# Layer 0 self attention: the causal mask is added on VectorE inside the instruction that takes the maximum, instead of by a product on TensorE, and the score units are regrouped

## The chip, the cores and the metric

One core of a Trainium2 chip runs the whole decoder in one launch. The metric is the device time of that launch in microseconds (us). The engines are called by their names in the profile: PE (TensorE), DVE (VectorE), ACT (ScalarE), POOL (GpSimd), SP (which here only issues DMAs).

## The reference

The program is a two-layer decoder on x[4, 1024, 256]; each layer has self attention, cross attention and a feed-forward part, each with a residual and a layer normalisation. The change lies in the first of these six parts:

```python
def _L0_attn_ref(x, w_in, b_in, w_out, b_out):       # E = 256, H = 16 heads of 16
    q, k, v = jnp.split(x @ w_in.T + b_in, 3, axis=-1)
    q, k, v = (to_heads(q), to_heads(k), to_heads(v))
    scores = jnp.einsum('bhqd,bhkd->bhqk', q * scale, k) + causal_bias   # 0 or -inf
    attn = jax.nn.softmax(scores, axis=-1)
    out = jnp.einsum('bhqk,bhkd->bhqd', attn, v)
    return out.transpose(0, 2, 1, 3).reshape(bsz, slen, esz) @ w_out.T + b_out
x = _layernorm(x + _L0_attn_ref(x, ...))
```

The softmax needs, for every query, the largest score among the keys that the query may see.

## The kernel before, in words

The self attention (`self_attention`) works through 16 head groups s: four batches of four groups, four heads each. K and Q of a group are spread by DMAs over 128 partitions, 32 for each head (16 rows of data), so that a matmul of one head uses 32 rows of PE and the four heads can run beside each other.

Each group is computed twice over. In the first pass (**a units**, tile `s<-kp,qp`) the scores are made with queries on the partitions, only to take the maximum of every query row, on DVE. `highest` (L356) joins a group's partial maxima `nmp` into `nmt` with the sign turned, `shifted_queries` (L366, L370) transposes `nmt` on PE and adds it to the spread queries as one more row, so that the second pass (**b units**, tile `s<-qs,kp`) yields scores from which the maximum has been subtracted. ACT takes exp of these (L399), POOL zeroes what lies above the diagonal (L402), and `weighted` multiplies with the values (tile `acc<-p,v`). `normalised`, `turned_back` and `out_projected` finish a batch.

The causal mask in the a units: for a query block qc of 128 rows, keys up to qc x 128 are needed whole, and the diagonal block of 128 x 128 with a mask that is 0 on and below the diagonal and -1e30 above. Before the change, `a_units` lists seven units without diagonal blocks, and two more units (u = 7 and 8) hold four diagonal blocks each:

```python
def after():
    for g in range(2):
        mm(t[g], ident_bf, cmask4.rearrange("p j n -> p (j n)"), False, True)
    for g in range(2):
        nc.vector.tensor_reduce(
            nmp[:, 2 * pair + g, q0 : q0 + 4, 0], t[g].rearrange("p (j n) -> p j n", j=4),
            AX.X, ALU.max,
        )
```

So the mask is added in PSUM by a product of the identity with four copies of the mask (bf16, 512 columns), and one reduction (L348) takes four maxima. The other units' maxima are taken by L332, one reduction for each piece of a PSUM bank: one of 512 columns (u = 0 to 3), or two of 384 + 128, 256 + 256 or 128 + 384 (u = 4 to 6). In this document a **split step** is one with such a unit of two pieces, a **full step** one with a single product of 512 columns.

The order of the work is written out by hand: `at(when, f, ...)` notes an event, and `run_in_order` runs them by their time, which only orders them. A group has 18 steps (9 units, two pairs of heads); `together` issues one a unit of group s and one b unit of group s - 1 for the other pair of heads, round by round, so that four matmuls of 32 rows stand next to each other. Before the change a group starts with its four diagonal steps, then come eight full and six split steps; the values products, transposes and projections stand between the steps. PE's instructions keep this order (`keep_in_program_order`); the other engines' instructions are ordered by the scheduler.

PSUM: the tiles `s` come from a pool of seven banks in rotation (`bank()`). Each step takes four (two for the a unit, two for the b unit), and each transpose, projection or values product one more. The outputs' projection (`out_projected`) leaves DVE a chain of five short instructions (L478, L481, L482, L136, L137) and, for every fourth block, the layer normalisation (L152, L169).

Of the kernel before, what the change touches and what calls it, by code (L numbers as in the profile page):

```python
# [8 lines left out]
F32 = mybir.dt.float32  # L9
BF16 = mybir.dt.bfloat16  # L10
U8 = mybir.dt.uint8
AF = mybir.ActivationFunctionType
ALU = mybir.AluOpType
AX = mybir.AxisListType
PSUM = bass.MemoryType.PSUM

P = 128
# [4 lines left out]
NC = S // P  # L22
# [7 lines left out]
def decoder_kernel(ctx: ExitStack, tc: tile.TileContext, a: dict, out: bass.AP):  # L30
    nc = tc.nc
# [60 lines left out]
    ident_bf = const.tile([P, P], BF16, tag="ident_bf", name="ident_bf")  # L92
# [3 lines left out]
    cmask = const.tile([P, P], BF16, tag="cmask", name="cmask")  # L96
# [89 lines left out]
    def self_attention(wk, pss, psa):  # L186
        def pe(ins):
            tc.keep_in_program_order(ins)

        def mm(o, l, r, start, stop):  # L190
            pe(nc.tensor.matmul(o, l, r, start=start, stop=stop))  # L191

        def bank():
            return pss.tile([P, 512], F32, tag="s", name="s")

        bq4 = wk.tile([P, 2], F32, tag="bq4", name="bq4", bufs=1)
        nc.vector.tensor_scalar(bq4, l0a_bq, 0.25, None, ALU.mult)
        cmask4 = wk.tile([P, 4, P], BF16, tag="cmask4", name="cmask4", bufs=1)
        for i in range(4):
            nc.vector.tensor_copy(cmask4[:, i, :], cmask)  # L200

        row16 = wk.tile([P, 1], F32, tag="row16", name="row16", bufs=1)
        nc.vector.tensor_reduce(
# [13 lines left out]
        for i in range(2):  # L217
            vt = wk.tile([P, NC, 17 * H + 16], F32, tag=f"v{i}", name=f"v{i}", bufs=1)
            nc.gpsimd.memset(vt, 1.0)
            vts.append(vt)  # L220
            nmp = wk.tile([P, 4, NC, 3], F32, tag=f"nmp{i}", name=f"nmp{i}", bufs=1)
            nc.gpsimd.memset(nmp, -3.0e38)
            nmps.append(nmp)
            nmt = wk.tile([P, NC, 4, 32], F32, tag=f"nmt{i}", name=f"nmt{i}", bufs=1)
            nc.gpsimd.memset(nmt, 0.0)
            nmts.append(nmt)

        bo2 = wk.tile([P, E], F32, tag="bo2", name="bo2", bufs=1)
        t = bank()
# [6 lines left out]
        def at(when, f, *args):  # L236
            events.append((when, len(events), f, args))
# [55 lines left out]
        def spread(kind, s):  # L293
# [8 lines left out]
        a_units = [  # L302
# [7 lines left out]
        ]  # L310

        def a_unit(s, u, pair):

            t = [bank() for _ in range(2)]
            qt, kt, nmp = qpads[s % 2], kpads[s % 3], nmps[s % 2]
            rows = [slice(64 * pair + 32 * g, 64 * pair + 32 * g + 32) for g in range(2)]
            rounds = []
            if u < 7:
                for qc, k0, n, c0 in a_units[u]:
                    rounds.append([  # L320
                        (
                            t[g][:, c0 : c0 + n], qt[rows[g], qc * P : (qc + 1) * P],
                            kt[rows[g], k0 : k0 + n], True, True,
                        )
                        for g in range(2)
                    ])

                def after():
                    for g in range(2):
                        for qc, k0, n, c0 in a_units[u]:  # L330
                            i = 2 if k0 else 1
                            nc.vector.tensor_reduce(  # L332
                                nmp[:, 2 * pair + g, qc, i : i + 1], t[g][:, c0 : c0 + n], AX.X, ALU.max
                            )
            else:
                q0 = 4 * (u - 7)
                for j in range(4):
                    cols = slice((q0 + j) * P, (q0 + j + 1) * P)
                    rounds.append([
                        (t[g][:, j * P : (j + 1) * P], qt[rows[g], cols], kt[rows[g], cols], j == 0, False)  # L340
                        for g in range(2)
                    ])

                def after():
                    for g in range(2):
                        mm(t[g], ident_bf, cmask4.rearrange("p j n -> p (j n)"), False, True)
                    for g in range(2):
                        nc.vector.tensor_reduce(  # L348
                            nmp[:, 2 * pair + g, q0 : q0 + 4, 0], t[g].rearrange("p (j n) -> p j n", j=4),
                            AX.X, ALU.max,  # L350
                        )

            return rounds, after

# [135 lines left out]
        for b in range(NB):  # L490
# [9 lines left out]
            for c in range(NC):  # L500
                u = (117.5, 135.5, 151.5, 155.5, 157.5, 171.5, 175.5, 177.5)[c]
# [13 lines left out]
        for s in range(4 * NB):  # L515
# [9 lines left out]
            for i, place in ((0, 6), (4, 14), (5, 16), (7, 22)):  # L525
                qh, kc = (0, 0) if i == 0 else (1, i - 3)
                n = 512 if (place + 1) % T in full[(s + 1 + place // T) % 4] else 384
# [13 lines left out]
        for s in range(4 * NB + 2):  # L541
            for j in range(18):
                units = []
                if s < 4 * NB:
                    units.append((a_unit, s, (7, 8, 0, 1, 2, 3, 4, 5, 6)[j // 2], 1 - j % 2))

                sb, jb = divmod(18 * (s - 1) + j - 2, 18)
                if 0 <= sb < 4 * NB:
                    units.append((b_unit, sb, jb // 2, jb % 2))
                if units:  # L550
                    at(s * T + 1 + j, together, *units)
# [3 lines left out]
    with (  # L555
        tc.tile_pool(name="l0a", bufs=2, reuse_waits="tile") as wk,
        tc.tile_pool(name="ps_l0a", bufs=7, space=PSUM, reuse_waits="tile") as pss,
        tc.tile_pool(name="ps_l0o", bufs=1, space=PSUM, reuse_waits="tile") as psa,
    ):
        self_attention(wk, pss, psa)  # L560
# [1093 lines left out]
```

## Time and profile before

| | |
|---|---|
| three runs | 2245.08, 2246.88 (median), 2253.66 us |
| the profiled execution | 2244.4 us |
| its span, first to last instruction | 2244.4 us |
| mean granted PE clock | 0.983 |
| layer 0 self attention | about 30 to 735 us of the span |
| period of a head group there (L356 to L356, mean of 15) | 42.75 us |
| one split or full step on PE, where nothing holds it | 1.07 us |
| L332, 512 / 384 / 256 / 128 columns | 684 / 550 / 416 / 282 ns, 640 instructions |
| L348, four maxima over 512 columns | 686 ns, 128 instructions |
| mask product on PE (96 of 128 recorded) | 392 ns each |

How to read it: the page's first part gives each engine's busy time as a share of the span. The groups of instructions name line, engine, operation, tiles (written <- read), shapes, count, busy time and the mean of one, and then the engine's idle time before them with what ended it. In the timeline, instructions of one kind that follow each other are merged: "1.42 ... x4" is four of them from the first start to the last end, and the bracket is the idle time of that engine just before, with its releaser. A DVE instruction is shown with its full duration, although the next may start some 80 ns before it ends. PE's ends are modelled, so steps are measured here from the start of one to the start of what follows.

### The profile page before, as it was taken

How to read it: one execution, taken by the hardware profiler on the slowest of the kernel's cores; microseconds unless marked ns; L12 is line 12 of the kernel's file. 1: busy time of each engine (PE TensorE's matmuls, PEld its weight loads, DVE VectorE, ACT ScalarE, POOL GpSimd, SP SyncE). 2: the span in 40 equal slices, each digit the busy share in tenths (PEclk: the TensorE clock that was granted, in tenths of full speed). 3: DMA queues.
4: the chain of work that ended last, by engine and by line, in shares of the span. 5: the costliest groups of instructions: out<-in, count | busy, mean ns of one | idle time of the engine just before them, and what ended most of it. 6: DMA issues, size and time to landing. Idle time of an engine off the chain costs nothing.

```text
span 2244.4 us, 38974 instructions
## 1 busy us (share of the span) xinstructions
PE 2120.4 (94%) x14676; PEld 1269.1 (57%) x14708; DVE 1492.5 (66%) x3287; ACT 1121.5 (50%) x2861; POOL 508.1 (23%) x1113
## 2 busy tenths in 40 slices
PE   7999999999999899999999998989999999999996
PEld 4544555554554556556556555666666655565554
DVE  5666667767775655558997887886973465555644
ACT  1455554555555365546756654454542234545443
POOL 1111111111111354444444443000000121111111
PEclk9999999999999999999999999999999999999998
DMA  4101100000000100000000000000000010010101
GB/s 115 34 6 53 39 6 16 15 11 15 11 11 1 39 1 20 1 1 1 1 1 1 34 1 22 0 1 1 1 1 1 2 20 15 15 29 10 29 1 37
DMA packets 24443, 34.83 MB, mean 16 GB/s; under 512 B 5952, under 2 KB 19648, under 8 KB 24256
## 3 DMA queue, kind: packets, MB, share of 16 engines
q1 hardware_dynamic: 22640, 31.20, 6.0%
q8 instruction: 116, 1.90, 0.3%
q10 hardware_dynamic: 1616, 1.16, 0.2%
q14 instruction: 71, 0.58, 0.1%
HBM read 15.56 MB, written 4.19 MB: 9 GB/s over the span
## 4 chain that ended last, share of the span: by engine, by line
PE 71%; DVE 19%; ACT 6%; issue 1%; POOL 1%; DMA 1%; SPq 0%; ACTq 0%; POOLq 0%; DVEq 0%
PE s L191 20%; PE t L590 16%; PE s L1190 10%; PE s L590 8%; PE acc L191 6%; DVE gt L940 4%; PE acc L1190 3%; PE t L774 2%; ACT u L749 2%; DVE nmp L332 2%; DVE x L169 1%; DVE nmx L745 1%; DVE bnst L136 1%; DVE ht L926 1%; DVE gt L950 1%
## 5 line engine op out<-in xcount | busy, mean ns | idle before, releaser
L399 ACT ACTIVATE p<-s 128x512 f32<-128x512 f32 x576 | 312.2, 595 | 292.4 <-PE s L191 284.2
L332 DVE TENSOR_REDUCE nmp<-s 128x1 f32<-128x512 f32 (+3 forms) x640 | 298.8, 523 | 153.7 <-PE s L191 152.9
L191 PE MATMUL s<-qs,kp 32*128 32x512 f32 (+3 forms) x1536 | 348.3, 522 | 0.0
L191 PE MATMUL s<-kp,qp 32*128 32x128 f32 (+3 forms) x2304 | 325.3, 404 | 2.4 <-DMA qp<-sq 2.1
L757 POOL TENSOR_SCALAR p<-u,rs 128x128 f32<-128x128 f32 x512 | 214.7, 437 | 292.3 <-DVE rs L753 199.9
L191 PEld LDWEIGHTS s<-kp,qp 32*128 32x128 f32 x2304 | 163.4, 187 | 135.2 <-ACT p L399 46.2
L402 POOL TENSOR_SCALAR_AFFINE_SELECT p<-p 128x256 f32<-128x256 f32 x256 | 99.5, 407 | 562.9 <-ACT p L399 562.9
L749 ACT ACTIVATE u<-s,nmx 128x154 f32<-128x154 f32 x512 | 192.0, 388 | 31.9 <-DVE nmx L745 27.9
L154 POOL TENSOR_TENSOR rstd<-ve,neghalf 128x4 f32<-128x4 f32 (+1 forms) x56 | 56.9, 1016 | 582.2 <-DVE ve L152 578.1
L191 PE MATMUL acc<-p,v 128*32 128x384 f32 (+3 forms) x2016 | 167.9, 420 | 0.1
L191 PEld LDWEIGHTS s<-qs,kp 32*128 32x128 f32 x1536 | 139.0, 184 | 29.1 <-DVE nmp L332 8.5
L590 PEld LDWEIGHTS s<-kt,qt 64*128 64x128 f32 x1024 | 102.5, 188 | 71.5 <-issue 53.6
L590 PE MATMUL s<-kt,qt 64*128 64x154 f32 x1024 | 136.2, 316 | 0.5 <-ACT qt L731 0.3
L590 PE MATMUL t<-xT,xw 128*128 128x512 f32 x256 | 123.2, 604 | 12.2 <-DVE xT L677 8.4
L745 DVE TENSOR_REDUCE nmx<-s 128x4 f32<-128x616 f32 x128 | 101.3, 791 | 48.4 <-PE s L590 48.2
L1347 DVE TENSOR_REDUCE nmt<-s 128x3 f32<-128x462 f32 (+1 forms) x192 | 99.0, 579 | 45.2 <-PE s L1190 45.1
L590 PE MATMUL t<-v,pt 128*128 128x256 f32 x512 | 118.0, 384 | 7.0 <-DVE pt L1099 7.0
L940 DVE SCALAR_TENSOR_TENSOR gt<-ht,cw,gt 128x256 f32<-128x256 f32 x256 | 116.9, 500 | 5.5 <-ACT gt L936 4.8
L590 PE MATMUL t<-xw,ot 128*128 128x256 f32 x512 | 116.3, 381 | 3.7 <-ACT pr L778 1.7
L590 PE MATMUL s<-qt,xT 128*128 128x512 f32 x256 | 116.8, 600 | 0.0
L590 PEld LDWEIGHTS t<-v,pt 128*128 128x128 f32 x512 | 97.0, 192 | 29.6 <-DVE pt L1099 8.1
L348 DVE TENSOR_REDUCE nmp<-s 128x4 f32<-128x512 f32 x128 | 82.4, 686 | 41.2 <-PE s L191 35.8
(259 smaller groups left out, 3892.2 us busy)
## 6 DMA issues: line engine op xcount, KB each, us to landing
qp<-sq SPq DMA_DIRECT2D x128, 64.0 KB, 2.4
kp<-sk SPq DMA_DIRECT2D x64, 64.0 KB, 2.3
out_dram<-x SPq DMA_DIRECT2D x8, 512.0 KB, 2.9
x<-in_x_dram SPq DMA_DIRECT2D x3, 1024.0 KB, 5.6
wf<-in_L_ffn_w_dram SPq DMA_DIRECT2D x2, 1024.0 KB, 6.0
xw<-in_L_xattn_wk_dram SPq DMA_DIRECT2D x1, 1024.0 KB, 6.4
xw<-in_L_xattn_wq_dram SPq DMA_DIRECT2D x1, 1024.0 KB, 5.0
xw<-in_L_xattn_wv_dram SPq DMA_DIRECT2D x1, 1024.0 KB, 5.0
```

Source lines behind the costliest of these rows:

```text
L191: pe(nc.tensor.matmul(o, l, r, start=start, stop=stop))
L332: nc.vector.tensor_reduce(nmp[:, 2 * pair + g, qc, i : i + 1], t[g][:, c0 : c0 + n], AX.X, ALU.max)
L348: nc.vector.tensor_reduce(nmp[:, 2 * pair + g, q0 : q0 + 4, 0], t[g].rearrange("p (j n) -> p j n", j=4), AX.X, ALU.max,)
L399: nc.scalar.activation(p[:, g, :], t[g], AF.Exp)
L402: nc.gpsimd.affine_select(out=v, in_=v, compare_op=ALU.is_ge, fill=0.0, base=0, pattern=[[0, 2], [1, P]], channel_multiplier=-1,)
L590: pe(nc.tensor.matmul(o, l, r, start=start, stop=stop))
L745: nc.vector.tensor_reduce(nmx.rearrange("p i g -> p g i"), t, AX.X, ALU.max, negate=True)
L749: nc.scalar.activation(u[:, 2 * i + g, :], t[:, g, i, :], AF.Exp, bias=nmx[:, i, g : g + 1], accum_out=ssum[:, i, g : g + 1],)
L757: nc.gpsimd.tensor_scalar(p[:, h * P : (h + 1) * P], u[:, h, :P], rs[:, h : h + 1], 1.0, ALU.mult, ALU.mult)
L940: nc.vector.scalar_tensor_tensor(g, ht[:, i, k : k + N], cw[:, hc, k : k + 1], g, ALU.mult, ALU.add)
L1190: pe(nc.tensor.matmul(o, l, r, start=start, stop=stop))
L1347: nc.vector.tensor_reduce(nmts[s % 2][:, 3 * u : 3 * u + n, g, 17], ts[g][:, : n * LK].rearrange("p (c k) -> p c k", k=LK), AX.X, ALU.max, ...
```

## The change

The mask product and its two units are gone. The a units are regrouped into nine that carry the diagonal block together with the keys before it: each piece that ends with the diagonal block is now read by one `tensor_tensor_reduce`, which adds a mask tile to the scores and takes the maximum in the same instruction. The mask tile `masked` is 384 columns of zeros followed by the 128 of the mask, in bf16, so that its last n columns fit a piece of n. The instruction also writes the sums, which nobody needs, to a bf16 tile `scratch` with a single buffer. `nmp` has two columns per query block instead of three. The units run in the order 0 to 8: six full ones (of which four without a diagonal block), then three of two pieces. The b units, their places and everything after them stay.

```diff
-        cmask4 = wk.tile([P, 4, P], BF16, tag="cmask4", name="cmask4", bufs=1)
-        for i in range(4):
-            nc.vector.tensor_copy(cmask4[:, i, :], cmask)
+        masked = wk.tile([P, 512], BF16, tag="masked", name="masked", bufs=1)
+        nc.vector.memset(masked[:, : 3 * P], 0.0)
+        nc.vector.tensor_copy(masked[:, 3 * P :], cmask)
...
-            nmp = wk.tile([P, 4, NC, 3], F32, tag=f"nmp{i}", name=f"nmp{i}", bufs=1)
+            nmp = wk.tile([P, 4, NC, 2], F32, tag=f"nmp{i}", name=f"nmp{i}", bufs=1)
...
             [(7, 0, 512, 0)],
-            [(7, 512, 384, 0), (1, 0, 128, 384)],
-            [(6, 512, 256, 0), (2, 0, 256, 256)],
-            [(5, 512, 128, 0), (3, 0, 384, 128)],
+            [(7, 512, 512, 0)],
+            [(3, 0, 512, 0)],
+            [(6, 512, 384, 0), (0, 0, 128, 384)],
+            [(2, 0, 384, 0), (4, 512, 128, 384)],
+            [(5, 512, 256, 0), (1, 0, 256, 256)],
         ]
...
+            def after():
+                for g in range(2):
+                    for qc, k0, n, c0 in a_units[u]:
+                        v = t[g][:, c0 : c0 + n]
+                        if k0 + n < (qc + 1) * P:
+                            nc.vector.tensor_reduce(nmp[:, 2 * pair + g, qc, 0:1], v, AX.X, ALU.max)
+                        else:
+                            scratch = wk.tile([P, 512], BF16, tag="scratch", name="scratch", bufs=1)
+                            nc.vector.tensor_tensor_reduce(
+                                scratch[:, :n], v, masked[:, 512 - n :], 1.0, -3.0e38, ALU.add, ALU.max,
+                                nmp[:, 2 * pair + g, qc, 1:2],
                             )
...
-                    for g in range(2):
-                        mm(t[g], ident_bf, cmask4.rearrange("p j n -> p (j n)"), False, True)
-                    for g in range(2):
-                        nc.vector.tensor_reduce(
-                            nmp[:, 2 * pair + g, q0 : q0 + 4, 0], t[g].rearrange("p (j n) -> p j n", j=4),
-                            AX.X, ALU.max,
-                        )
...
-                    units.append((a_unit, s, (7, 8, 0, 1, 2, 3, 4, 5, 6)[j // 2], 1 - j % 2))
+                    units.append((a_unit, s, j // 2, 1 - j % 2))
```

An entry of `a_units` is (query block, first key, columns, place in the bank).

More of the change, by code (lines that the diff above doesn't have):

```diff
@@ L317, in a_unit @@
             rounds = []
[L318 to L323, printed above, removed]
-                        )
-                        for g in range(2)
-                    ])
-                def after():
-                    for g in range(2):
[L330 to L333, printed above, removed]
-                            )
[L335 to L344, printed above, removed]
-                    for g in range(2):
-                        mm(t[g], ident_bf, cmask4.rearrange("p j n -> p (j n)"), False, True)
-                    for g in range(2):
-                        nc.vector.tensor_reduce(
-                            nmp[:, 2 * pair + g, q0 : q0 + 4, 0], t[g].rearrange("p (j n) -> p j n", j=4),
-                            AX.X, ALU.max,
-                        )
@@ new lines, in a_unit @@
+            for qc, k0, n, c0 in a_units[u]:
+                rounds.append([
+                    (
+                        t[g][:, c0 : c0 + n], qt[rows[g], qc * P : (qc + 1) * P],
+                        kt[rows[g], k0 : k0 + n], True, True,
+                    )
+                    for g in range(2)
+                ])
+            def after():
+                for g in range(2):
+                    for qc, k0, n, c0 in a_units[u]:
+                        v = t[g][:, c0 : c0 + n]
[6 more added lines that the diff above has]
+                                nmp[:, 2 * pair + g, qc, 1:2],
+                            )
```

## The prediction

> **What bounds the kernel now.** I read the page's busy times first, then the groups of line L191 by shape, then the timeline of one head group (about 42.7 us) on PE and on DVE, and last the waits of PE. Only the stage from about 30 to 735 us changes, the self attention of layer 0. There PE is busy nearly without a break and DVE is not:
>
> ```profile
> PE 2120.4 (94%) x14676; PEld 1269.1 (57%) x14708; DVE 1492.5 (66%) x3287; ACT 1121.5 (50%) x2861; POOL 508.1 (23%) x1113
> ```
> ```profile
> 250.00:650.00 400.00, 392.02 (x3843) 205.19 (x3858) 280.89 (x618) 209.47 (x384) 59.91 (x148) 1.00 0.09 17
> ```
>
> The second line is the window 250 to 650 us: PE 392 of 400 us, DVE 281 (70%), ACT 209. So the stage is PE's, and DVE has some 30% to spare on the average. An average hides where the spare time lies, so here is DVE in a stretch that the change touches: one head group's six split steps (two products per bank), without output projections beside them.
>
> ```profile
> 170.10 1.42 DVE L332 TENSOR_REDUCE nmp<-s 128x1 f32<-128x384 f32 x4 [0.88 <-PE s L191]
> 173.09 1.42 DVE L332 TENSOR_REDUCE nmp<-s 128x1 f32<-128x384 f32 x4 [1.57 <-PE s L191]
> 174.94 1.42 DVE L332 TENSOR_REDUCE nmp<-s 128x1 f32<-128x256 f32 x4 [0.44 <-PE s L191]
> 176.77 1.42 DVE L332 TENSOR_REDUCE nmp<-s 128x1 f32<-128x256 f32 x4 [0.41 <-PE s L191]
> 178.66 1.42 DVE L332 TENSOR_REDUCE nmp<-s 128x1 f32<-128x128 f32 x4 [0.47 <-PE s L191]
> 180.48 1.42 DVE L332 TENSOR_REDUCE nmp<-s 128x1 f32<-128x128 f32 x4 [0.41 <-PE s L191]
> 181.93 0.26 DVE L356 TENSOR_REDUCE nmt<-nmp 128x32 f32<-128x96 f32 x1
> ```
>
> The bracket is DVE's idle time before a group: after one long gap only 0.41 to 0.47 us per step are free. At the end stands L356, which gathers the maxima of the head group; PE transposes its result (L366), and cannot go on before. In groups with two output projections that wait is there already:
>
> ```profile
> PE s L366 <- DVE nmt L356: 9.2, 6, 2.4
> ```
>
> **What goes from PE.** A step is one score unit of the group (two matmuls per round) beside one unit of the exponentials of the group before. Of the 18 steps of a group, four are diagonal blocks with the mask product behind them. A diagonal step and, for comparison, the first lines of the two steps around it on PE:
>
> ```profile
> 306.06 0.38 PE L191 MATMUL s<-kp,qp 32*128 32x128 f32 x2
> ...
> 307.13 1.07 PE L191 MATMUL acc<-p,v 128*32 128x512 f32 x8
> ...
> 311.06 0.38 PE L191 MATMUL s<-kp,qp 32*128 32x128 f32 x2
> ...
> 312.16 0.60 PE L191 MATMUL s<-cmask,ident_bf 128*128 128x512 bf16 x2
> 312.69 1.06 PE L191 MATMUL acc<-p,v 128*32 128x512 f32 x8
> ```
>
> The split step takes 307.13 - 306.06 = 1.07 us, a diagonal one 312.69 - 311.06 = 1.63 (1.53 where a transpose follows: 308.13 to 309.66). Full steps of 512 columns also take 1.07 (293.68 to 294.75 holds 512 columns of each kind). After the change the four diagonal steps are four more full steps, the split steps stay six, and the columns stay 9 x 512 per pair. So PE saves 0.46 to 0.56, mean 0.51 us, in 64 steps: **-33 us** at most. The two products and two loads of the identity per step go with it; that is the whole of it, no DMA moves.
>
> **What DVE gets.** The number of instructions that take maxima is unchanged (48 per group over the same 18,432 columns), but 32 of the 48 become the combined one, and in the built program's order each of those is two instructions: the combined one, and one that writes its accumulator to the 128x1 result. Only the second signals, so the PSUM bank is given back by it, and, as the scratch output has one buffer, each next combined instruction waits for it. No row shows either. I price them by neighbours:
> - The combined pass over 512 elements: like a two-source pass from PSUM (L370, 681 ns each, two in 1.28) against 684 and two in 1.29 of the reduction. Equal, 0.
> - The accumulator read and the wait: the nearest row is a 128x2 statistic (L137) followed by an instruction that waits for it (L152), at 348.21 and 348.42 in the timeline: 0.216 us from start to start.
> So +0.216 per combined instruction. From below: a small instruction with no wait behind it (L137 at 302.94, the next instruction at 303.04) takes 0.10. From above: ACT's accumulator read (L1087, 193 ns) with 0.038 for a wait and 0.050 for a separate wait instruction (as at L370), and the slowest two-source row over 512 elements (L1469, 748 instead of 681): 0.35. I take 0.216, the row with the same shape of dependence.
>
> [...]
>
> **Where the price lands.** Of the six full units per pair four (u = 0 to 3) hold no diagonal block and keep the plain reduction: no cost in 8 steps. The other four full steps (u = 4, 5) get 2 x 0.216 = 0.43 on 1.29 of DVE time, beside steps that come every 2.2 us: hidden, except that the bank comes back 0.22 later where PE already stalls on it (321.34 to 323.23 takes 1.89 instead of 1.07). I put 0.2 us per group, **+3**. The six split steps get 4 x 0.216 = 0.86 each, 5.18 per group, on gaps of 0.4: they become DVE's. A gap can swallow only what came before it, so of the first gap (1.57, behind one step) 0.86 is used and the rest of the gaps in full. Then L356 moves, and PE's transposes with it, less the slack they have now (mostly 0.5 or 0). By the timelines of the sixteen groups, each named by the start of its split steps:
> - 85, 168, 211: gaps used 2.6, L356 later by 2.6, less 0.5 slack: 2.1 each, 6.2. 125 (two long gaps): 0.7.
> - 252, 428, 605 (one projection): used 2.66, 2.5 later, no slack: 7.5. 293, 470: used 2.86, 2.3 less 0.5: 3.6.
> - 339, 385, 515, 562 (two projections): used 1.3, 3.9 later, no slack: 15.6.
> - 645: 3.5; 684: 4.4; the first, 46, where DVE has no gap: 5.1.
> Sum **+46.6**. Against it stand three diagonal steps of each group, those after the transposes: 48 x 0.51, and the very first one: **-25**; the one before the transposes saves nothing where PE waits there anyway. Last, seven banks turn over: a step takes four, and where a projection or value product takes one between, the step's last matmul needs the second bank of the step before, which DVE returns 0.86 later. Followed by hand through the group of 252, PE then delivers late and DVE idles 0.85 once; the transposes come 3.2 instead of 2.5 later. I take 0.4 per group, **+6**.
>
> Sum: 46.6 - 25 + 6 + 3 = **+31 us** on the profiled execution's 2244.4: 2275. The median of the three runs, 2246.9, lies 2.5 above that execution; so 2277.
>
> **Rivals.**
> 1. *The read is cheap and the cover holds* (faster, 0.20). At 0.10 per instruction a split step grows 0.4, which the 0.41 to 0.47 gaps just hold. L356 is then late only in groups with projections (four by 1.6, three by 0.8) and in 46, 645 and 684 (together 5.2): +12 with -2 from the others, against -25: -13, so 2234; at no price at all -33, 2214. For it: DVE is at 70%. Against it: the 0.216 row. Between -13 at 0.10 and +31 at 0.216 both sides are equal near 0.135; below that this rival decides.
> 2. *It cancels* (0.13): a price of 0.12 to 0.16, about 2250.
> 3. *The combined pass runs at half speed* (0.07): two streams and a sum, then a running maximum. An element takes 1.05 ns in L332 (684 - 282 over 384 elements). The combined pass reads 10,240 elements per group, 6,144 of them in the split steps: 6.4 us more there, all bound, and I allow 1.5 for the rest: 7.9 x 16 = 126 on top of 31, so 2403. L370 and L926 (two sources, 512 elements, 681 and 678 ns) speak against it. [...]
> My forecast lies on the slow side, so rival 1 is the one with the other sign.
>
> **Numbers.** Forecast 0.60 at 2277; rivals 0.20, 0.13, 0.07. About 0.5% (11 us) is what measurement of this kernel can tell. Faster 0.20, same 0.13, slower 0.67. The price's ends give 2234 (0.10) and, at 0.35, 24 x 0.134 x 16 = 51 more, 2328. So the forecast's own range is 2258 to 2328, and the range over all cases 2228 to 2330; below it lies the free case, above it the half-speed one.
>
> **What would show it.** Right: the mask product gone from L191's groups and steps of 1.07 in the first four places; accumulator reads of 150 to 190 ns, 512 of them; start to start of combined pairs near 0.82 at 512 elements; split steps 2.2 us apart on DVE with no gaps; L366's wait for L356 grown from 9 to some 45 us. Wrong: gaps remain in the split steps, or a combined pair takes 0.7 (rival 1) or over 1.2 (rival 3); or the stage falls to under 700 us.

## The result and the profile after

The changed kernel takes **2264.9 us** (median of 4 runs, 2262.6 to 2268.0) against 2248.8 (2245.1 to 2253.7): ratio **1.0071**, 95% interval 1.005 to 1.0091. It is slower by 16 us, where 31 were forecast. The profiled execution took 2268.0 us, its span 2266.1, the mean granted PE clock fell from 0.983 to 0.972. Nearly the whole loss lies in the stage that was changed. Of the 21.7 us between the two profiled spans, 16.3 are there at its last L345 (`nmt`, L356 before), which starts at 716.2 us instead of 699.9, and 19.9 at the stage's last matmul (764.83 instead of 744.97).

In the changed kernel the plain reduction is L334, the combined instruction and its accumulator read are L337, `highest` is L345, the transposes L355 and the shifted queries L359.

First the busy times of the whole span, from the first part of the page, and then the window from 250 to 650 us (PE, PEld, DVE, ACT, POOL, then the clock):

```profile
PE 2124.3 (94%) x13812; PEld 1256.6 (55%) x13812; DVE 1526.7 (67%) x3797; ACT 1121.4 (49%) x2861; POOL 507.4 (22%) x1113
```
```profile
250.00:650.00 400.00, 380.03 (x3268) 193.44 (x3265) 293.45 (x892) 204.69 (x375) 59.19 (x146) 0.98 0.09 16
```

PE was busy 392 of these 400 us and is now busy 380: 20 us of idleness where there were 8. DVE rose only from 281 to 293, far from full. As averages these lines would call PE the bound and DVE free. The waits of PE in the stage (30 to 766 us; sum, count, longest) say where the 12 us went:

```profile
PE s L355 <- DVE nmt L345: 28.8, 12, 4.3
PE s L355 <- ACT p L388: 5.3, 4, 1.4
```

Both are the same wait, before the transposes at the end of each head group; in four groups another event happens to come last by the profile, although `nmt` is late there too. It held PE for 9.2 us before and for 34.1 now. What makes `nmt` late is seen on DVE, in the split steps of the group whose timeline the prediction showed:

```profile
177.49 0.56 DVE L337 CUSTOM_DVE_ANT_0 scratch<-s,masked 128x384 bf16<-128x384 f32 x1 [1.04 <-PE s L191]
177.97 0.08 DVE L337 DVE_READ_ACCUMULATOR2_ANT nmp<- 128x1 f32 x1
178.09 0.29 DVE L337 CUSTOM_DVE_ANT_0 scratch<-s,masked 128x128 bf16<-128x128 f32 x1
178.31 0.08 DVE L337 DVE_READ_ACCUMULATOR2_ANT nmp<- 128x1 f32 x1
178.53 0.56 DVE L337 CUSTOM_DVE_ANT_0 scratch<-s,masked 128x384 bf16<-128x384 f32 x1
179.02 0.08 DVE L337 DVE_READ_ACCUMULATOR2_ANT nmp<- 128x1 f32 x1
179.13 0.29 DVE L337 CUSTOM_DVE_ANT_0 scratch<-s,masked 128x128 bf16<-128x128 f32 x1
179.35 0.08 DVE L337 DVE_READ_ACCUMULATOR2_ANT nmp<- 128x1 f32 x1
179.58 0.56 DVE L337 CUSTOM_DVE_ANT_0 scratch<-s,masked 128x384 bf16<-128x384 f32 x1
...
187.82 0.22 DVE L345 TENSOR_REDUCE nmt<-nmp 128x32 f32<-128x64 f32 x1
```

The four pieces of a step start 0.60, 0.44, 0.60 and 0.45 us apart, 2.09 us for a step whose four plain reductions took 1.42, and behind the bracket (idle time) at 177.49 none is left up to L345. From an accumulator read to the next combined instruction it is 0.12 us where that one waits for the read alone, 0.22 where it waits for PE as well. From the first split step to L345 it was 11.83 us (170.10 to 181.93) and is 13.32 for the same steps here (174.50 to 187.82).

The gain on PE is there too. Two of the three steps behind the transposes that had diagonal blocks, each from its first matmul to what follows, on PE:

```profile
189.62 0.70 PE L191 MATMUL s<-kp,qp 32*128 32x512 f32 x2
...
190.70 1.07 PE L191 MATMUL acc<-p,v 128*32 128x512 f32 x8
191.69 0.70 PE L191 MATMUL s<-kp,qp 32*128 32x512 f32 x2
...
192.77 1.99 PE L191 MATMUL s<-qkv,xT 128*128 128x256 f32 x8
```

1.08 us each, where a diagonal step took 1.63. No mask product stands between.

To put sizes on it I cut every head group at the starts of its 18 steps, and took the mean time from one step's start to the next over groups 1 to 14 (all the work between them counts, so a step is longer here than its matmuls). The fourth and fifth columns are two experiments told below:

| us per group | before | after | no mask in the maximum | pieces apart in the scratch tile |
|---|---|---|---|---|
| first step, and behind it the wait and the transposes | 3.64 | 5.16 | 3.48 | 3.67 |
| the three steps behind them, diagonal ones before | 8.00 | 6.72 | 6.87 | 6.76 |
| eight full steps | 18.00 | 18.24 | 17.99 | 18.18 |
| six split steps | 13.43 | 13.61 | 13.44 | 13.46 |
| sum | 43.07 | 43.73 | 41.78 | 42.07 |

So PE gains 1.28 us in three steps of a group and loses 1.52 in the first, which holds the wait.

### The profile page after: what moved, and what is told of

The parts are those of the page before. It is cut to its first block, busy times and chain, and to the rows that moved or that the text cites. A ratio compares the mean times of both kernels' runs of the same rounds, so it can differ in the third digit from the quotient of the medians.

```text
span 2266.1 us, 38034 instructions
## 1 busy us (share of the span) xinstructions
PE 2124.3 (94%) x13812; PEld 1256.6 (55%) x13812; DVE 1526.7 (67%) x3797; ACT 1121.4 (49%) x2861; POOL 507.4 (22%) x1113
## 4 chain that ended last, share of the span: by engine, by line
PE 70%; DVE 20%; ACT 6%; issue 1%; POOL 1%; DMA 1%; SPq 0%; DVEq 0%; ACTq 0%; POOLq 0%
PE s L191 19%; PE t L579 15%; PE s L1179 10%; PE s L579 8%; PE acc L191 6%; DVE gt L929 4%; PE acc L1179 3%; DVE scratch L337 3%; PE t L763 2%; ACT u L738 2%; DVE x L169 1%; DVE nmx L734 1%; DVE bnst L136 1%; PE s L355 1%; DVE ht L915 1%
## 5 line engine op out<-in xcount | busy, mean ns | idle before, releaser
L191 PE MATMUL s<-qs,kp 32*128 32x512 f32 (+3 forms) x1536 | 356.5, 528 | 0.3 <-DVE nmp L337 0.3
L191 PE MATMUL s<-kp,qp 32*128 32x512 f32 (+3 forms) x1536 | 331.6, 535 | 2.2 <-DMA qp<-sq 1.9
L337 DVE CUSTOM_DVE_ANT_0 scratch<-s,masked 128x256 bf16<-128x256 f32 (+3 forms) x512 | 250.8, 490 | 102.3 <-PE s L191 64.0
L334 DVE TENSOR_REDUCE nmp<-s 128x1 f32<-128x512 f32 x256 | 164.0, 684 | 71.4 <-PE s L191 71.1
L191 PEld LDWEIGHTS s<-kp,qp 32*128 32x128 f32 x1536 | 129.2, 189 | 144.1 <-ACT p L388 48.2
L191 PEld LDWEIGHTS s<-qs,kp 32*128 32x128 f32 x1536 | 145.3, 188 | 42.3 <-issue 8.4
```

What stands on the lines that cost most here:

```text
L334: nc.vector.tensor_reduce(nmp[:, 2 * pair + g, qc, 0:1], v, AX.X, ALU.max)
L337: nc.vector.tensor_tensor_reduce(scratch[:, :n], v, masked[:, 512 - n :], 1.0, -3.0e38, ALU.add, ALU.max, nmp[:, 2 * pair + g, qc, 1:2],)
```

## The experiments

The theory: PE's gain is real, and DVE's price in the split steps, 0.19 us per combined instruction, is paid at one place, PE's wait for `nmt`. Rivals: the regrouping itself costs; banks that come back late cost; DVE's total time costs. Later a second question came up: is the price the accumulator read, or the wait of each combined instruction for the one before it? All times are medians with the range of the runs, ratios are to the kernel before, run on the same chip (its medians there: 2247.5 to 2249.1).

### What the change is worth without DVE's part

```diff
-                        if k0 + n < (qc + 1) * P:
-                            nc.vector.tensor_reduce(nmp[:, 2 * pair + g, qc, 0:1], v, AX.X, ALU.max)
-                        else:
...
+                        i = int(k0 + n == (qc + 1) * P)
+                        nc.vector.tensor_reduce(nmp[:, 2 * pair + g, qc, i : i + 1], v, AX.X, ALU.max)
```

> The changed kernel with a plain reduction in every place: the mask is left out of the maximum (the exponentials are still masked afterwards). PE does what it does after the change, DVE what it did before. Theory A, the time of the combined instructions on DVE in the split steps makes the maxima late: PE's wait at the transposes returns to about 10 us in all (34 after the change), the gain of the three diagonal steps behind it stays (-19 us), and the others gain a little: 2218 to 2230 us. Rival, the regrouping itself (six full units, the heavier pieces last) is what costs: the wait stays over 20 us and the time above 2240.

Measured: 2228.9 us (2224.3 to 2230.2), ratio 0.9915 (0.9899 to 0.9931), inside the expected range. Against it, the kernel before without its mask product, everything else left:

```diff
-                        (t[g][:, j * P : (j + 1) * P], qt[rows[g], cols], kt[rows[g], cols], j == 0, False)
+                        (t[g][:, j * P : (j + 1) * P], qt[rows[g], cols], kt[rows[g], cols], True, True)
...
-                    for g in range(2):
-                        mm(t[g], ident_bf, cmask4.rearrange("p j n -> p (j n)"), False, True)
```

> The kernel before without the mask product on PE: the mask is left out of the maximum, all else stays, the diagonal units with four blocks of 128 columns too. Theory A says that PE's time in this stage is what ends it, so the 64 products pairs' 0.4 to 0.55 us each show, less what bank turnover holds back: -20 to -28 us, 2220 to 2228. Rival: the product was hidden beside other waits and its removal gives less than 8 us.

Measured: 2230.1 us (2225.9 to 2230.5), ratio 0.9916 (0.9901 to 0.9932), 2 us above the range that was expected of it. The two agree within 1.2 us, so the regrouping by itself neither gains nor costs anything that these runs can tell, and that rival is out. Three steps then make up the change: the product leaves PE, -18; the units are regrouped, -1; the combined instruction comes to DVE, 2264.9 - 2228.9 = **+36**. By the table above 23.5 us of these 36 lie in the first steps of groups 1 to 14, which hold the wait (5.16 against 3.48), and by the traces 7.2 in the first group (28.45 us instead of 21.30). Some of the gain on PE is taken at once by the wait for `nmt`, with plain reductions too:

```profile
PE s L349 <- DVE nmt L339: 14.0, 9, 3.0
```

That is the kernel without the mask in its maximum: 14.0 us, 4.8 more than the 9.2 before. PE got faster, and so comes earlier to a result that does not.

### Where the price is paid: the order of the units

```diff
-                    units.append((a_unit, s, j // 2, 1 - j % 2))
+                    units.append((a_unit, s, (6, 7, 8, 4, 5, 0, 1, 2, 3)[j // 2], 1 - j % 2))
```

> The changed kernel with its split units first and the four plain full units last in each group; every instruction stays, only where it stands changes. Theory A: the last steps before the gathering of the maxima are now light on DVE (1.29 us on steps of 2.2), so PE's wait at the transposes falls from 34 us to under 8; the split steps at the start of a group are bound by DVE or by its banks for 0.5 to 1 us per group: 2245 to 2255 us, 10 to 20 below the changed kernel. Rival B, banks come back late with the accumulator read: the stalls move along with the split steps, 2260 to 2270. Rival C, DVE's total time counts: no change, 2265.

Measured: **2239.2 us** (2235.8 to 2241.4), ratio 0.996 (0.9946 to 0.9975). With the same instructions and the same DVE time (1521 us busy instead of 1527) the kernel is 25.7 us faster, more than each theory expected. Of the wait this is left:

```profile
PE s L355 <- DVE nmt L345: 5.5, 4, 2.2
```

So with the same DVE time the loss depends on where that time falls, and the total alone is out as the cause. Not all of the 25.7 us is DVE's price, though: the kernel without the mask in its maximum gains 15.5 by the same order (2228.9 to 2213.4, below), so the price goes from 36 to 25.8 (2239.2 - 2213.4). Nor did all of the 28.6 us of waits come back as time: the split steps now stand at the transposes, where DVE also has the shifted queries to make, and with the wait and the transposes among them the six take 15.09 us per group. The same order without the mask in its maximum (below) takes 13.94 there, so 1.15 us per group of DVE's price are still paid. Whether they are paid by banks returned late isn't shown.

The same idea on the kernel before, as a control:

```diff
-                    units.append((a_unit, s, (7, 8, 0, 1, 2, 3, 4, 5, 6)[j // 2], 1 - j % 2))
+                    units.append((a_unit, s, (4, 5, 6, 7, 8, 0, 1, 2, 3)[j // 2], 1 - j % 2))
```

> The kernel before, mask product and plain reductions kept, only its units in another order: the split ones first, then the two diagonal ones, then the full ones. A control for the order. If the order helps only by giving DVE time before the transposes, it can save here no more than the wait that is there, 9.5 us: 2238 to 2246. If the order is worth something in itself (banks, exponentials), it gives here what it gave the changed kernel, some 25 us: 2222.

Measured: 2237.5 us (2236.1 to 2238.9), ratio 0.9941 (0.9924 to 0.9958): 11 us gained, not 25, at the edge of the range that the wait allows. But the wait there only fell from 9.2 to 5.6 us:

```profile
PE s L366 <- DVE nmt L356: 5.6, 4, 2.2
```

So most of these 11 us is not that wait. The kernel without the mask in its maximum shows the same: the order gives it 15.5 us, while its wait falls by 8.5 (14.0 to 5.5). The order is worth some 7 to 8 us (an estimate, 11.4 - 3.6 and 15.5 - 8.5) besides the wait; what they are is not shown.

The counterpart: 16 more combined instructions per group, in steps that have time for them.

```diff
-                            nc.vector.tensor_reduce(nmp[:, 2 * pair + g, qc, 0:1], v, AX.X, ALU.max)
+                            scratch = wk.tile([P, 512], BF16, tag="scratch", name="scratch", bufs=1)
+                            nc.vector.tensor_tensor_reduce(
+                                scratch[:, :n], v, masked[:, 0:1].to_broadcast([P, n]), 1.0, -3.0e38, ALU.add, ALU.max,
+                                nmp[:, 2 * pair + g, qc, 0:1],
+                            )
```

> The changed kernel, and the eight full steps of a group that had plain reductions use the combined instruction as well (with a column of zeros as its second operand, so nothing else is computed): 16 more combined instructions per group, 256 in all, each with its accumulator read and its wait. By the rate of the changed kernel's full steps (0.235 us more than the plain one) DVE is busy and waiting 256 x 0.235 = 60 us longer. If only the split steps matter, because the full steps' work on DVE (2 x 0.85 = 1.7 us) fits into steps that come every 2.2 us, the time moves by +3 to +8 us over the changed kernel: 2268 to 2273. If DVE's total time sets the loss, wherever it lies, it is +35 us or more: above 2300.

Measured: 2277.9 us (2276.4 to 2280.7), ratio 1.0124 (1.0106 to 1.0142): 13 us above the changed kernel. That is neither the 3 to 8 of my theory nor the 35 and more of the rival. The 60 us were too many as well: only the second of a full step's two pieces waits inside the step, and the 128 full steps in question grew from 1.29 to 1.54 us each, 33 us in all. 13 us for 33 is about the share that the changed kernel loses (36 for some 88: 96 split steps x 0.75 and 64 full ones x 0.25, an estimate), so this run alone doesn't separate the two; the order above, with the same DVE time and a price of 25.8 instead of 36, does. The wait before the transposes is no longer than it was (28.0 + 5.3 us), so these 13 us are paid elsewhere: per group 0.4 us in the three steps behind the transposes and 0.4 in the eight full ones, and 1.8 in the first group. The cover of the full steps is not perfect, which counts against my term for them.

### The read or the wait

In the first try the combined instruction writes its sums back to its own piece of the PSUM bank, so that no scratch tile stands between it and the next:

```diff
-                            scratch = wk.tile([P, 512], BF16, tag="scratch", name="scratch", bufs=1)
...
-                                scratch[:, :n], v, masked[:, 512 - n :], 1.0, -3.0e38, ALU.add, ALU.max,
+                                v, v, masked[:, 512 - n :], 1.0, -3.0e38, ALU.add, ALU.max,
```

> The changed kernel, but the combined instruction writes its sums back to the PSUM piece it read, so no scratch tile makes the next one wait; the accumulator reads stay. Theory A with the price split into read (0.08 us) and wait (0.04 to 0.15): start to start at 512 elements falls from 0.845 to about 0.70 us, a split step from 2.07 to 1.8, the wait at the transposes from 34 to 18 to 25 us, the time to 2248 to 2256. Rival: the accumulator read alone carries the price, and nothing changes, 2262 to 2268.

Measured: 2240.5 us (2236.8 to 2242.6), ratio 0.9966 (0.9954 to 0.9978). It gained 24.4 us, more than I gave the wait and far more than the rival. The passes are longer there (713 ns for 512 columns instead of 690) and the reads too (141 ns instead of 83), and still it is faster: the next pass starts together with the read (169.85, 170.37 and 170.62 us in the first split step of a group). But writing into PSUM is a second difference. So the next one changes which columns of the scratch tile are written; the tile is also made once and not anew for every instruction. The instructions and their bytes stay:

```diff
+        scratch = wk.tile([P, 512], BF16, tag="scratch", name="scratch", bufs=1)
...
-                            scratch = wk.tile([P, 512], BF16, tag="scratch", name="scratch", bufs=1)
...
-                                scratch[:, :n], v, masked[:, 512 - n :], 1.0, -3.0e38, ALU.add, ALU.max,
+                                scratch[:, c0 : c0 + n], v, masked[:, 512 - n :], 1.0, -3.0e38, ALU.add, ALU.max,
```

> The changed kernel with one scratch tile for all, in which each combined instruction writes at the columns that its piece has in the bank (384 + 128, 256 + 256), not at column 0. The two pieces of a bank then no longer overlap, so a combined instruction in a split step waits for the accumulator read two before it, which is long done, and not for the one just before; the full steps keep their wait. The number of instructions, of reads and of bytes is that of the changed kernel, and nothing is written into PSUM. If the wait on the instruction just before is the price, the split steps shrink as in the form that writes in place (start to start of two 256 column pieces from some 0.47 to 0.38 to 0.43 us) and the time falls to 2238 to 2248. If the accumulator read itself is the price and writing in place gained by something else, 2258 to 2266.

Measured: **2238.3 us** (2237.9 to 2240.5), ratio 0.996 (0.9946 to 0.9974), as the wait predicts. A split step of it on DVE:

```profile
172.82 0.42 DVE L337 CUSTOM_DVE_ANT_0 scratch<-s,masked 128x256 bf16<-128x256 f32 x1 [0.40 <-PE s L191]
173.17 0.08 DVE L337 DVE_READ_ACCUMULATOR2_ANT nmp<- 128x1 f32 x1
173.17 0.42 DVE L337 CUSTOM_DVE_ANT_0 scratch<-s,masked 128x256 bf16<-128x256 f32 x1
173.51 0.08 DVE L337 DVE_READ_ACCUMULATOR2_ANT nmp<- 128x1 f32 x1
173.51 0.42 DVE L337 CUSTOM_DVE_ANT_0 scratch<-s,masked 128x256 bf16<-128x256 f32 x1
173.86 0.08 DVE L337 DVE_READ_ACCUMULATOR2_ANT nmp<- 128x1 f32 x1
173.86 0.42 DVE L337 CUSTOM_DVE_ANT_0 scratch<-s,masked 128x256 bf16<-128x256 f32 x1
174.20 0.08 DVE L337 DVE_READ_ACCUMULATOR2_ANT nmp<- 128x1 f32 x1
174.64 0.42 DVE L337 CUSTOM_DVE_ANT_0 scratch<-s,masked 128x256 bf16<-128x256 f32 x1 [0.36 <-PE s L191]
```

The next combined instruction now starts together with the read (173.17, 173.51, 173.86). The read costs next to nothing; the step takes about 1.46 us (172.82 to 174.28), and gaps (the brackets) are back. That the tile is made only once is not what took the waits away: in a full step of the same kernel, where both pieces write all 512 columns, the second still waits.

```profile
196.24 0.69 DVE L337 CUSTOM_DVE_ANT_0 scratch<-s,masked 128x512 bf16<-128x512 f32 x1 [0.79 <-PE s L191]
196.86 0.08 DVE L337 DVE_READ_ACCUMULATOR2_ANT nmp<- 128x1 f32 x1
197.09 0.69 DVE L337 CUSTOM_DVE_ANT_0 scratch<-s,masked 128x512 bf16<-128x512 f32 x1
```

It starts 0.23 us behind the read, as in the changed kernel (0.84 us from pass to pass in both). So of the 36 us that the combined instruction cost, 2264.9 - 2238.3 = **26.6** are the waits in the split steps alone. What is left is 2238.3 - 2228.9 = 9.4. By the traces 3.3 us of it lie in the first group, and by the table 2.7 in the first steps with the wait and 2.7 in the eight full steps of groups 1 to 14. That these come from the waits left in the full steps is likely, but not shown.

### Both cures together

In each of these the units stand in the order with the split ones first. In place:

> The changed kernel with both earlier edits: the combined instruction writes its sums back into its own piece of the PSUM bank (no scratch buffer between one and the next), and the three split units of a group come first, the six full ones behind them. If the loss is the one wait of PE for the maxima before its transposes, both edits take away the same wait (34 us in the changed kernel, 19.6 left in place, 5.5 left by the order), so their gains of 24.4 and 25.7 us don't add up: I expect 2230 to 2238, with under 4 us left of that wait. If the two edits cure different losses (the order the banks, the place of the sums the time of DVE), they add up: 2264.9 - 24.4 - 25.7 = about 2215. If DVE's writes into PSUM hold PE up at the banks it reads beside them, it is not below 2239.

Measured: 2225.1 us (2222.3 to 2228.3), ratio 0.9889 (0.987 to 0.9907). That lies between my range and the sum of both gains, and my reason was wrong: 5.5 us of the wait stay, not under 4, and they stay in every version with this order, without the mask as well, so they aren't the combined instruction's. What I left out is that the order alone had moved part of its loss to the steps behind the transposes (12.15 us per group in the five split steps there), and a shorter split step saves some of that too (11.44).

With the pieces apart in the scratch tile:

> The same with the split units first in each group. Writing in place and this order together gave 2225.1. If that came from the shorter split steps and nothing that is special to writing into PSUM, 2223 to 2232 here; if only the order is left to work, 2237 to 2241, as with the order alone.

Measured: **2218.9 us** (2216.8 to 2219.1), ratio **0.9871** (0.9854 to 0.9889), below the range. It keeps the mask in the maximum as the changed kernel does, and beats both kernels: 30 us under the one before. The six split steps take 14.06 us, where the order alone gave 15.09 and the same order without the mask in the maximum 13.94, so most of what the order had moved there was DVE's waits and not the place. That writing into PSUM brought the gain is out as well.

And the ideal, without the mask in the maximum:

> The changed kernel with plain reductions everywhere (the mask is left out of the maximum; the exponentials are still masked), and with the split units first. It joins the two ideal halves: no price on DVE, and no split steps before the transposes. With plain reductions in the changed order 2228.9 was measured, with 14 us of waits for the maxima; if these are what is left to win, 2215 to 2223. If the order costs something by itself (late banks after the transposes), 2226 to 2232.

Measured: 2213.4 us (2211.2 to 2216.1), ratio 0.9836 (0.9815 to 0.9856), just under the range. DVE's price, 36 us in the changed kernel, is 5.5 us here (2218.9 - 2213.4).

The last try at those:

```diff
-                                scratch[:, c0 : c0 + n], v, masked[:, 512 - n :], 1.0, -3.0e38, ALU.add, ALU.max,
+                                v if g and n == 512 else scratch[:, c0 : c0 + n], v, masked[:, 512 - n :], 1.0, -3.0e38, ALU.add, ALU.max,
```

> The fastest version so far that keeps the mask in the combined instruction (pieces at their own columns of the scratch tile, split units first: 2218.9 us), and its last waits on the instruction just before taken away as well: of the two combined instructions of a full step, which would both write all 512 columns of the scratch tile, the second now writes back to its own PSUM bank. Without any price on DVE this order took 2213.4. If the wait in the full steps is what is left, 2213 to 2217; if it is covered there, or if writing into PSUM costs as much as it saves (writing all sums back took 2225.1, 6 us more than the scratch tile), 2218 to 2222.

Measured: 2216.4 us (2208.1 to 2217.7), ratio 0.9847 (0.9826 to 0.9869). The two passes of a full step now start 0.62 us apart instead of 0.84, so the wait is gone. But the interval overlaps that of 2218.9, so a gain isn't settled, nor is the cause of the last 5 us.

## Why the prediction was right, and where its sizes were off

The direction, the mechanism and its place were right: PE gains in the diagonal steps, DVE is late in the split ones, and the bill comes at the transposes. Its sizes were too big on both sides. By the experiments the gain is 18 and the price on DVE 36; the prediction had 25 against 46.6 + 6 + 3 = 56. The two errors, 7 and 20 us, have opposite signs and partly cancel, which was luck; what is left is 31 forecast against 16 measured. By the traces, before against after:

- **The gain on PE, -25.** Summed over groups 1 to 15 the three steps behind the transposes gain 19.0 us, 0.42 a step and not 0.51. About 1.6 of the missing 4 us lie at the clock (last section): in the groups behind the four longest waits these steps are that much longer than in groups of the same kind. The rest is not explained; the first of the three steps gains 0.54 us, the second 0.31, the third 0.43.
- **The transposes, +46.6.** Measured 22.4 in groups 1 to 15, 3.9 in the first group as a whole, what PE gains in it included (5.1 in the prediction, where DVE was said to have no gap, before that gain), and 2.6 at the last one: 29. Two inputs were off. The price of 0.216 stands for the first piece of a bank (0.843 - 0.608 = 0.235 for 512 columns, read from the starts), but a second piece, which waits for DVE alone, costs less; a step of four grew from 1.34 (1.42 less the 0.08 by which the next may start early) to 2.09, so 0.19 each. And the gaps of 0.41 to 0.47 were counted from the end of the last reduction, although the next may start 0.08 before that. With 0.75 per step and 0.08 more in each gap the group of 168 is 5 x 0.75 - (0.44 + 0.41 + 0.47 + 0.41 + 4 x 0.08) = 1.7 us late, where the prediction had 2.6; measured were 1.5.
- **Banks, +6 in the split steps and +3 in the full ones.** Measured +2.5 and +3.4.
- **The lower bound of the price.** I bounded the price from below by 0.10, a small instruction with no wait behind it. Without the wait the read costs next to 0: the next instruction starts with it. Had the pieces not shared columns of a scratch tile, rival 1 would have had the right side (2234 at 0.10, 2214 at none; 2238.3 was measured with waits left in the full steps, and 2228.9 with no price at all, since PE's gain is 18 and not 33).
- **The wait itself.** Two 256-element steps in a chain start 0.45 us apart in the kernel before (L478 at 301.11, L481 at 301.56), four reductions of 256 elements that don't wait for each other 0.335 (1.42 us together). In the changed kernel too the wait is what costs: 0.12 us from a read to a piece that waits for it, against 0.00 to 0.02 without the wait (the pieces apart in the scratch tile), and 26.6 us of the kernel's time between the split steps with such waits and without.
- **Rival 3, half speed,** did not happen: 690 ns for 512 columns against 684 of the plain reduction. Rival 2, that it cancels, had a price of 0.12 to 0.16 and 3 us; with 0.19 the 16 us lie about halfway between it and the forecast.
- **What would show it.** 512 reads, no gaps in the split steps and 0.843 us from one 512 column pair to the next came as said. A read takes 83 ns and not 150 to 190, a split step 2.09 and not 2.2, and the wait grew to 34 and not 45.

## What to carry to other kernels

Before moving work from a full engine to one with spare time, find the step in which that engine's result is waited for, and move the work to the other end of the period if the order allows: here that was worth 26 us with the same instructions, of which some 10 are the price of the moved work and 15.5 came without it as well. Look at what an instruction writes that nobody reads: here a scratch tile with one buffer made each combined instruction wait for the one before it, and giving neighbours different columns cost nothing and won 27 us. A price taken from a row that shares the same dependence was good to 15%. In the group of 168, where 2.6 us were forecast and 1.5 measured, 0.6 of the error is that price and 0.3 that it was added to gaps measured differently from the durations.

## What the runs showed of the hardware

**A wait of PE can cost more than its length.** Between 300 and 700 us the granted clock of the changed kernel fell to half four times, for 3.4 us each, every time at or just behind the end of one of the four longest waits there (4.0, 2.7, 4.0 and 2.7 us). In the kernel before, whose longest wait there is 1.9, it did not fall. First the transposes after a wait of 1.30 us and what follows them, then those of a group with 4.05 us:

```profile
188.19 1.06 PE L355 MATMUL s<-ident,nmt 128*128 128x128 f32 x8 [1.30 <-ACT p L388]
189.09 0.60 PE L440 MATMUL s<-ident,ot 128*128 128x128 f32 x4
189.62 0.70 PE L191 MATMUL s<-kp,qp 32*128 32x512 f32 x2
...
362.08 1.78 PE L355 MATMUL s<-ident,nmt 128*128 128x128 f32 x8 [4.05 <-DVE nmt L345]
363.65 1.06 PE L440 MATMUL s<-ident,ot 128*128 128x128 f32 x4
364.64 1.19 PE L191 MATMUL s<-kp,qp 32*128 32x512 f32 x2
...
366.20 1.07 PE L191 MATMUL acc<-p,v 128*32 128x512 f32 x8
```

From the transposes to the first step it is 1.43 us in one and 2.56 in the other, and that step takes 1.08 and 1.56: 1.6 us more, behind a wait of 4. The window from 362.27 to 365.69 us has clock 0.50. How long a wait must be is not fixed. In the kernel without the mask in its maximum two waits of 2.41 us stand in groups of the same kind; behind the one at 341 us nothing is slower, behind the one at 513 us the clock halves (windows: length, then busy times, and the clock as the first number after them):

```profile
510.90:514.30 3.40, 1.11 (x10) 1.14 (x11) 3.36 (x10) 1.08 (x2) 0.76 (x2) 1.00 0.23 39
514.30:517.70 3.40, 3.40 (x21) 1.58 (x22) 2.49 (x6) 0.59 (x2) 0.00 (x0) 0.51 0.03 5
```

PE was busy for 1.11 of the 3.40 us before the clock fell. A long wait is not the only occasion either: in the first head group of the changed kernel the clock fell to half at 55.07 us, where PE had been busy for 3.29 of the 3.42 us before. Why is not shown.

**The accumulator of DVE.** Reading it is an instruction of 83 ns that the next pass overlaps (its start is 0.00 to 0.02 us behind the read's), unless that pass waits for it (0.12). Behind a pass that writes f32 to PSUM it takes 141 ns, overlapped as well. A combined pass with one f32 source in PSUM and one bf16 source in SBUF runs nearly as fast as the plain reduction: 690, 556, 422 and 291 ns for 512, 384, 256 and 128 columns against 684, 550, 416 and 282.
